# A Mamba scan layer and a Fourier layer on one core: the ends of the scan, and forward transforms by pairs of columns

## The chip, the cores and the metric

The kernel runs on one core of one Trainium2 chip. The metric is the device time of one execution in microseconds (us), as the median of several runs. A profile of one further execution gives the start and end of every instruction on the engines: PE (TensorE matmul; PEld is its weight load), DVE (VectorE), ACT (ScalarE), POOL (GpSimd) and SP (the queue that issues most DMAs).

## The reference

The input is x of shape 4 x 128 x 128 x 128 (image, channel, x, y), all float32. Layer 0 cuts each image into windows of 8 x 8 pixels, normalizes over channels, and runs a selective state-space scan over the 64 pixels of each window:

```python
t = x.reshape(B, C, nh, WS, nw, WS).transpose(0, 2, 4, 3, 5, 1).reshape(-1, L, C)
tn = (t - mu) * jax.lax.rsqrt(var + 1e-05) * ln_g + ln_b
xz = tn @ W_in + b_in
xi, z = (xz[..., :d_in], xz[..., d_in:])
xc = silu(sum((xp[:, k:k + L, :] * conv_w[:, k] for k in range(K))) + conv_b)
delta = jax.nn.softplus(dr @ dt_w + dt_b)
h = dA * h + (d_t * x_t)[:, :, None] * B_t[:, None, :]
y = jnp.einsum('nds,ns->nd', h, C_t)
```

Layer 1 normalizes again, takes a real two-dimensional Fourier transform, multiplies by conjugated filters, transforms back, mixes channels and ends in a small MLP:

```python
Xf = jnp.fft.rfft2(z, axes=(-2, -1))
Uf = Xf[:, :, None, :, :] * jnp.conj(Phi)[None, None]
U = jnp.fft.irfft2(Uf, s=(gx, gy), axes=(-2, -1))
S = jnp.einsum('bdlxy,lhd->bhxy', U, Theta)
```

## The kernel before

Four functions run one after another, joined by tensors in DRAM. All are scheduled by hand: each engine executes its instructions in the order in which the program text issues them, and the framework adds the waits that data and buffers need. DMAs are nearly all issued from SP's queue, which is in order too: a DMA that waits for its data or its buffer holds up all DMAs behind it.

**`mamba_layer` (from L34).** The 4 x 16 strips of 8 rows of pixels are called rows here, 64 in all. First come constants (L59 to L125): 17 loads over SP, the folding of the convolution into W_in (`W_conv`, L86 to L106) and of two projections into `W_dt` (L108 to L116), each through the only buffer of the PSUM tag `one`, and memsets of four `dA` tiles and `tn` on DVE. Then everything runs over slots `s` (L446): a row has U = 32 slots of the scan, one unit of 128 x 1024 elements in each, and its forward part starts LEAD = 30 slots ahead. The dictionaries `takes`, `makes` and `lates` say which helper runs in which slot. For the row that starts at `s`, these are the normalization of `xt` (`norm`, L293: matmul `ln_center`, ACT work `ln_scale`, matmul `ln_back`, ACT `f_affine`, for two halves in turn), convolutions and inputs (`f_conv`, `f_in`), Silu (`f_silu`, with a load of activation tables on either side), `f_dt`, `f_bc`, softplus (`f_soft`), the product `du`, and the stores of `delta` and `du` to DRAM, from which `fetch` loads replicated copies (`dr`, `ur`) for the scan. After the scan of a row come the gate, `b_out`, the store of `x1t`, a second normalization 89 slots after `s`, and the store of `z`.

PSUM has eight banks: three tiles of two banks under the tag `du` for the scan, one bank `y` for its sums, and the one bank `one`, through which every other matmul result passes.

For the first row nothing else runs while its forward part does; for the last row nothing else runs while its output and second normalization do.

**`spectra` (from L464).** For each of the four images: `along_x` (L493) multiplies, for each channel, a 128 x 128 plane `z` with the 128 columns of `fx` (cosines, then sines, of frequencies 0 to 64), four channels to a PSUM bank, and copies the bank into `a`, on ACT and DVE in turn. `z` arrives by tiles of 16 channels (512 KB) with three buffers, two loads ahead. Then `along_y` (L500) forms the spectrum column by column, three columns to a bank: column k needs the real part `a[:, m]` times one pair of blocks of `fy` and the imaginary part `a[:, WH + m]` times another, summed in PSUM, where m is k or 128 - k. Real and imaginary halves are then copied by ACT and DVE into `x`, 65 frequencies 512 bytes apart:

```python
nc.tensor.matmul(p2[:, o], a[:, m], fy[:, KY : 3 * KY], start=True, stop=single)
if not single:
    by = fy[:, : 2 * KY] if m == k else fy[:, 2 * KY :]
    nc.tensor.matmul(p2[:, o], a[:, WH + m], by, start=False, stop=True)
```

After each half of the 128 columns `x` (two buffers) is stored to `xf`, 4.26 MB (L527). The PSUM tags `p1` and `p2` have four banks each.

**`mix` (L530) and `images_and_mlp` (L616)** multiply by `phi` and `theta` and transform back. They read the constants `Phi_r`, `Phi_i` and `idft_x`, made in `layout` (L773) and `dft` (L745), in the order of the 128 columns.

Of the kernel before, what the change touches and what calls it, by code (L numbers as in the profile page):

```python
# [32 lines left out]

def mamba_layer(tc, d, x, x1, zb, deltas, dus):  # L34
# [18 lines left out]
    with ExitStack() as ctx:  # L53
# [4 lines left out]

        def load(name):  # L59
            t = cp.tile(list(d[name].shape), F32, tag=name, name=f"c_{name}")  # L60
            nc.sync.dma_start(t, d[name])
            return t
# [10 lines left out]
        names = "center rsel ssel ln_g ln_b W_in b_in conv_w conv_b W_bc dt_b A_log D W_out b_out gamma beta"  # L73
        c = {k: load(k) for k in names.split()}
        A = cp.tile([P, 32], F32, tag="A", name="A")
# [8 lines left out]
        fold = sb.tile([P, n], F32, tag="ab", name="fold")  # L84
        nc.sync.dma_start(fold[:, : 2 * P], d["W_in_t"])
        for ch in range(2):  # L86
            nc.vector.tensor_scalar(skip[:, ch], ident, c["D"][:, ch : ch + 1], None, ALU.mult)
            t = ps.tile([P, HB], F32, tag="one", name="p_fold")
            for k in range(K):
                diag = half(fold, 1)[:, k * P : (k + 1) * P]  # L90
                nc.vector.tensor_scalar(diag, ident, c["conv_w"][:, ch, k : k + 1], None, ALU.mult)
                w = fold[:, ch * P : (ch + 1) * P]
                nc.tensor.matmul(t[:, k * P : (k + 1) * P], w, diag, start=True, stop=True)
            nc.vector.tensor_copy(W_conv[:, ch].rearrange("p k m -> p (k m)"), t)

            b = c["b_in"][:, ch : ch + 1]
            sums = fold[:, 2 * P : 2 * P + K]
            nc.vector.tensor_copy(sums[:, :1], c["conv_w"][:, ch, :1])
            for k in range(1, K):
                nc.vector.tensor_tensor(sums[:, k : k + 1], sums[:, k - 1 : k], c["conv_w"][:, ch, k : k + 1], ALU.add)  # L100
            nc.vector.tensor_scalar(sums, sums, b, None, ALU.mult)
            for k in range(K - 1):
                nc.vector.tensor_scalar(
                    early[:, ch, :, k], sums[:, K - 2 - k : K - 1 - k].to_broadcast([P, WS]), -1.0, None, ALU.mult
                )
            nc.vector.tensor_tensor(b_conv[:, ch : ch + 1], sums[:, K - 1 :], c["conv_b"][:, ch : ch + 1], ALU.add)  # L106

        W_dt = cp.tile([P, 2, 2 * P], F32, tag="W_dt", name="W_dt")  # L108
        fold = sb.tile([P, n], F32, tag="ab", name="fold2")
        nc.sync.dma_start(fold[:DR, : 2 * P], d["W_xdt"])  # L110
        nc.sync.dma_start(fold[:DR, HB : HB + 2 * P], d["dt_w"])
        for ch in range(2):
            t = ps.tile([P, HB], F32, tag="one", name="p_fold")
            w = fold[:DR, ch * P : (ch + 1) * P]
            nc.tensor.matmul(t[:, : 2 * P], w, fold[:DR, HB : HB + 2 * P], start=True, stop=True)
            nc.vector.tensor_copy(W_dt[:, ch], t[:, : 2 * P])  # L116

        dAs = []
        for i in range(4):
            t = cp.tile([P, 2, WS, L], F32, tag=f"dA{i}", name="dA")  # L120
            nc.vector.memset(t, 0.0)
            dAs.append(t)

        tn = cp.tile([P, NW, K - 1 + L], F32, tag="tn", name="tn")
        nc.vector.memset(tn, 0.0)  # L125

        def one(name):
            return ps.tile([P, HB], F32, tag="one", name=name)

        rs = [SimpleNamespace(py={}, yz={}) for _ in rows_all]  # L130
# [14 lines left out]
        def ln_center(o, src, h):  # L145
            o.ln = one("ln_cen")
            for q in range(HB // P):
                at = h * HB + q * P
                tokens = getattr(o, src)[:, at : at + P]
                nc.tensor.matmul(o.ln[:, q * P : (q + 1) * P], tokens, c["center"], start=True, stop=True)  # L150

        def ln_scale(o):
            o.cs = sb.tile([P, HB], F32, tag="cs", name="cs", bufs=2)
            r = sb.tile([P, HB // P], F32, tag="ln_r", name="ln_r", bufs=2)
            blocks = [slice(q * P, (q + 1) * P) for q in range(HB // P)]
            for q, k in enumerate(blocks):
                nc.scalar.activation(o.cs[:, k], o.ln[:, k], AF.Square, accum_out=r[:, q : q + 1])

            nc.scalar.activation(r, r, AF.Ln, bias=eps, scale=1.0 / P)
            nc.scalar.activation(r, r, AF.Exp, scale=-0.5)  # L160
            for q, k in enumerate(blocks):
                nc.scalar.activation(o.cs[:, k], o.ln[:, k], AF.Copy, scale=r[:, q : q + 1])  # L162

        def ln_back(o):
            o.lb = one("ln_back")
            for q in range(HB // P):
                k = slice(q * P, (q + 1) * P)
                nc.tensor.matmul(o.lb[:, k], o.cs[:, k], ident, start=True, stop=True)  # L168


        def f_load(o, b, rows):
            o.xt = sb.tile([P, n], F32, tag="xt", name="xt", bufs=3)
            nc.sync.dma_start(o.xt, x[b, :, rows, :].rearrange("c i w -> c (i w)"))
# [119 lines left out]
        def norm(o, src, affine, at):  # L293
            for h in range(2):
                made(at + 2 * h, partial(ln_center, o, src, h), partial(ln_scale, o))
                made(at + 2 * h + 1, partial(ln_back, o), partial(affine, o, h))
# [3 lines left out]
        for r, (o, (b, rows)) in enumerate(zip(rs, rows_all)):  # L300
            s = U * r - LEAD
            for h in range(2):
                for k in range(2):
                    late(s + LEAD + 16 * h + 8 * k + 11, partial(b_gate, o, h, k))
                made(s + (61, 67)[h], partial(b_out, o, h), partial(b_out_bias, o, h))
            take(s + 72, partial(b_store, o, b, rows))
            norm(o, "x1t", b_affine, s + 89)
            take(s + 96, partial(b_store_z, o, b, rows))
        for r, (o, (b, rows)) in enumerate(zip(rs, rows_all)):
            s = U * r - LEAD  # L310
            take(s - 5, partial(f_load, o, b, rows))
            norm(o, "xt", f_affine, s - 1)
# [133 lines left out]
        for s in range(-LEAD - 5, U * R + 99 - LEAD):  # L446
            make, took = makes.get(s, ((), ()))
            go(takes.get(s, ()))
            fetch(s + 6)
            if s % 2:  # L450
                replicate(s + 1)
            else:
                total(s - 4)
            for q in range(2):
                decay(s + 2, q, True)
            for q in range(2):
                decay(s + 3, q, False)
            go(make)
            go(took)
            scan(s)  # L460
            go(lates.get(s, ()))


def spectra(tc, d, zb, xf):  # L464
# [10 lines left out]
    with ExitStack() as ctx:  # L475
# [3 lines left out]
        ps = ctx.enter_context(tc.tile_pool(name="f_ps", bufs=4, space=PSUM))  # L479
        fx = cp.tile([P, W], F32, tag="fx", name="fx")  # L480
        nc.sync.dma_start(fx, d["dft_x"])
        fy = cp.tile([P, 4 * KY], F32, tag="fy", name="fy")
# [4 lines left out]
        def load(b, i):  # L487
            b, i = b + i // P, i % P
            if b < B:
                loaded[b, i] = sb.tile([P, DG, W], F32, tag="z", name="z", bufs=3)  # L490
                nc.sync.dma_start(loaded[b, i], zb[b][i : i + DG].rearrange("c x y -> x c y"))

        def along_x(b, i, a):  # L493
            z = loaded[b, i - i % DG]
            p1 = ps.tile([P, CG, W], F32, tag="p1", name="p_fx")
# [3 lines left out]

        def along_y(a, x, cols):  # L500
            p2 = ps.tile([P, KG, 2 * KY], F32, tag="p2", name="p_fy")
            for o, k in zip(range(KG), cols):
                m = min(k, W - k)
                single = m % WH == 0
                nc.tensor.matmul(p2[:, o], a[:, m], fy[:, KY : 3 * KY], start=True, stop=single)
                if not single:
                    by = fy[:, : 2 * KY] if m == k else fy[:, 2 * KY :]
                    nc.tensor.matmul(p2[:, o], a[:, WH + m], by, start=False, stop=True)
            n, at = len(cols), cols[0] % WH
            for r in range(2):  # L510
                next(copies)(
                    x[:, :, r, at : at + n].rearrange("p y k -> p k y"), p2[:, :n, r * KY : (r + 1) * KY]
                )

        load(0, 0)
        load(0, DG)
        for b in range(B):
            a = sb.tile([P, W, P], F32, tag="a", name="a", bufs=1)
            for i in range(0, P, CG):
                if i % DG == 0:  # L520
                    load(b, i + 2 * DG)
                along_x(b, i, a)
            for q in range(2):
                x = sb.tile([P, KY, 2, WH], F32, tag="x", name="x")
                for k in range(q * WH, (q + 1) * WH, KG):
                    along_y(a, x, range(k, min(k + KG, (q + 1) * WH)))
                nc.sync.dma_start(xf[:, :, b, q].rearrange("y c r x -> c y r x"), x)  # L527
# [217 lines left out]
def dft():  # L745
# [7 lines left out]
        "dft_y": (h.imag, h.real, -h.imag, -h.real),  # L753
        "idft_x": (w.real, w.imag),
# [18 lines left out]
def layout(i):  # L773
# [17 lines left out]
    d["Phi_r"], d["Phi_i"] = (i[f"L1_conv_Phi_f_{k}"].transpose(1, 0, 2) for k in ("real", "imag"))  # L791
# [21 lines left out]
```

## Time and profile before

| what | us |
|---|---|
| median of three runs | 10317.22 (10314.53 to 10325.69) |
| the profiled execution | 10328.0 |
| its span, first to last instruction | 10326.2 |
| start of the first scan instruction | 107.06 |
| end of the last scan instruction | 7163.65 |
| issue of the last store of `z` | 7190.91 |
| issue of the last store of `xf` | 7602.14 |
| first matmul of the mix | 7628.4 |
| first matmul of the inverse transforms | 9529.0 |

So the scan layer takes some 7191 us, of which 107 before the first scan and 27 after the last, the forward transforms 411 to the issue of their last store, the mix some 1900 and the rest some 800. Over the whole span PE is busy for 9221.1 us (89%), DVE 8861.2 (86%), POOL 8141.9 (79%), ACT 6509.4 (63%). Such shares are averages over stages with different limits; a stage is read from its own stretch of the trace. In the groups of instructions that follow, a line holds the source line, the engine and operation, the tile written and the tiles read, the shape and count, then busy time in us and the mean of one in ns, and after it the idle time of that engine just before the group, with what ended it.

### The profile page before, as it was taken

The page shows a single profiled execution, that of the slowest core. Times are in us where ns is not written, and L with a number is a line of the kernel's source. Part 1 is how long each engine was busy: PE and PEld are TensorE (multiplying, and loading weights), DVE is VectorE, ACT ScalarE, POOL GpSimd, SP SyncE. Part 2 cuts the span into 40 slices and gives each one's busy share as a digit, 9 for nine tenths or more (in the row PEclk, how much of TensorE's full clock was granted, in tenths as well). Part 3 has the DMA queues.
Part 4 walks back from the last instruction along what each step waited for, and adds up shares of the span by engine and source line. Part 5 has one row for each costly group of instructions (what it writes and reads, how often), then busy time and mean ns, then how long its engine had stood idle before and what let it go on. Part 6 is the DMA issues. An engine that isn't in the chain of part 4 may idle for free.

```text
span 10326.2 us, 144410 instructions
## 1 busy us (share of the span) xinstructions
PE 9221.1 (89%) x48900; PEld 5007.4 (48%) x48900; DVE 8861.2 (86%) x7193; ACT 6509.4 (63%) x12439; POOL 8141.9 (79%) x4166
## 2 busy tenths in 40 slices
PE   6888888888888888888888888887889999998999
PEld 2333333333333333333333333333889999998766
DVE  5999999999999999999999999997359999998433
ACT  5777777777777776776776776775335555554433
POOL 5889999899899899899898899996039999996000
PEclk8999999999999999999999999997999999999999
DMA  4777777777777677677677777776531111112332
GB/s 141 222 219 220 220 221 219 217 222 219 217 225 221 212 232 218 212 230 219 211 227 220 210 227 220 214 226 183 154 103 38 38 38 38 38 38 62 138 127 94
DMA packets 1168115, 1794.11 MB, mean 174 GB/s; under 512 B 368640, under 2 KB 436496, under 8 KB 1166224
## 3 DMA queue, kind: packets, MB, share of 16 engines
q1 hardware_dynamic: 1167376, 1784.88, 57.1%
q8 instruction: 388, 6.36, 0.3%
q14 instruction: 351, 2.88, 0.1%
HBM read 1481.44 MB, written 303.04 MB: 173 GB/s over the span
## 4 chain that ended last, share of the span: by engine, by line
PE 65%; ACT 15%; DVE 8%; DMA 7%; issue 3%; SPq 1%; POOL 1%; DVEq 0%; ACTq 0%; POOLq 0%
PE p_v L564 18%; PE p_conv L202 6%; PE p_du L376 6%; DVE hs L410 5%; DMA dr<-delta 5%; PE p_dt L227 5%; PE p_bc L217 5%; PE p_y L428 5%; PE p_out L274 2%; DVE p_du L408 2%; ACT dA L391 2%; PE ln_cen L150 2%; ACT p_du L391 2%; PE p_h L686 2%; PE p_o L695 2%
## 5 line engine op out<-in xcount | busy, mean ns | idle before, releaser
L418 POOL TENSOR_TENSOR hs<-hs,bc 128x1024 f32<-128x1024 f32 x2048 | 4801.2, 2366 | 413.6 <-DVE hs L410 359.7
L410 DVE TENSOR_TENSOR_SCAN hs<-dA,p_du 128x1024 f32<-128x1024 f32 x1600 | 3659.0, 2287 | 208.6 <-DVE p_du L408 4.9
L581 POOL TENSOR_TENSOR acc<-acc,part 128x512 f32<-128x512 f32 x1408 | 1740.9, 1280 | 570.9 <-ACT part L579 565.9
L408 DVE TENSOR_TENSOR p_du<-p_du,bc 128x1024 f32<-128x1024 f32 x1600 | 1936.0, 1210 | 224.0 <-PE p_du L376 219.2
L391 ACT ACTIVATE dA<-dr,A 128x504 f32<-128x504 f32 x3200 | 2071.8, 704 | 32.9 <-DVE hs L410 23.3
L564 PE MATMUL p_v<-theta,xk 128*128 128x128 f32 x16640 | 1864.8, 275 | 31.5 <-DMA xk<-xf 27.0
L564 PEld LDWEIGHTS p_v<-theta,xk 128*128 128x128 f32 x16640 | 1861.9, 192 | 34.4 <-issue 27.2
L592 DVE SCALAR_TENSOR_TENSOR acc<-p_v,phi,acc 128x512 f32<-128x512 f32 x2622 | 1767.8, 743 | 105.4 <-PE p_v L564 80.9
L376 PE MATMUL p_du<-du,c_rsel 32*128 32x512 f32 x6400 | 1365.3, 678 | 369.9 <-DVE hs L410 369.9
L428 PE MATMUL p_y<-hs,c_ssel 128*32 128x512 f32 x8192 | 1223.7, 633 | 135.1 <-DVE yz L263 83.3
L579 ACT ACTIVATE part<-p_v,phi 128x512 f32<-128x512 f32 x1408 | 891.1, 686 | 578.7 <-PE p_v L564 572.0
L410 DVE TENSOR_TENSOR_SCAN hs<-p_du,ur 128x1024 f32<-128x1024 f32 x448 | 1019.0, 2275 | 87.1 <-ACT p_du L391 52.7
L356 POOL TENSOR_TENSOR ur<-ur,bc 128x1024 f32<-128x1024 f32 x448 | 1059.8, 2366 | 10.8 <-DMA ur<-du 10.8
L202 PE MATMUL p_conv<-tn,W_conv 128*128 128x512 f32 x2048 | 1010.8, 618 | 3.2 <-ACT xc L207 1.6
L376 PEld LDWEIGHTS p_du<-du,c_rsel 32*128 32x128 f32 x6400 | 370.7, 192 | 1081.0 <-issue 783.2
L227 PE MATMUL p_dt<-xc,W_dt 128*128 128x512 f32 x1024 | 620.3, 736 | 46.8 <-ACT dl L238 40.9
L391 ACT ACTIVATE p_du<-dr,A 128x504 f32<-128x504 f32 x896 | 613.8, 685 | 29.0
L428 PEld LDWEIGHTS p_y<-hs,c_ssel 128*32 128x32 f32 x8192 | 184.3, 111 | 890.3 <-issue 572.2
L207 ACT ACTIVATE xc<-p_conv,b_conv 128x512 f32<-128x512 f32 x256 | 176.2, 688 | 645.2 <-PE p_conv L202 645.2
L245 POOL TENSOR_TENSOR dl<-dl,ab 128x1024 f32<-128x1024 f32 x128 | 302.1, 2360 | 340.0 <-ACT ab L242 340.0
L202 PEld LDWEIGHTS p_conv<-tn,W_conv 128*128 128x128 f32 x2048 | 348.0, 190 | 457.5 <-issue 249.4
L168 PE MATMUL ln_back<-ident,cs 128*128 128x128 f32 x2048 | 339.5, 316 | 224.4 <-ACT cs L162 218.4
(99 smaller groups left out, 10104.8 us busy)
## 6 DMA issues: line engine op xcount, KB each, us to landing
dr<-delta SPq DMA_DIRECT2D x4096, 256.0 KB, 5.2
ur<-du SPq DMA_DIRECT2D x896, 256.0 KB, 6.4
delta<-dl SPq DMA_DIRECT2D x128, 512.0 KB, 2.9
du<-du SPq DMA_DIRECT2D x128, 512.0 KB, 5.2
xf<-x SPq DMA_DIRECT2D x8, 4160.0 KB, 16.4
xk<-xf SPq DMA_DIRECT2D x130, 256.0 KB, 3.7
sf<-acc SPq DMA_DIRECT2D x520, 64.0 KB, 1.7
s<-sf SPq DMA_DIRECT2D x8, 4160.0 KB, 12.6
```

Of the source, the lines that this page charges most:

```text
L202: nc.tensor.matmul(windows(o.pc), W_conv[:, ch, k], moved, start=(k == 0), stop=(k == K - 1))
L227: nc.tensor.matmul(o.pd, W_dt[:, k, ch * P : (ch + 1) * P], half(o.xc[:, k], h), start=(k == 0), stop=(k == 1))
L356: nc.gpsimd.tensor_tensor(fetched[s], fetched[s], both(o.bc[0], h), ALU.mult)
L376: nc.tensor.matmul(u.bank[:, j % 2], c["rsel"][p, u.i], half(u.o.du[p, u.ch], u.h), start=True, stop=True)
L391: nc.scalar.activation(u.dA[:, q, :, 1:], u.delta[:, q].rearrange("p (w t) -> p w t", t=L)[:, :, 1:], AF.Exp, scale=A[:, g : g + 1],)
L408: nc.vector.tensor_tensor(u.bu, u.bu, both(u.o.bc[0], u.h), ALU.mult)
L410: nc.vector.tensor_tensor_scan(u.hs.rearrange("p q t -> p (q t)"), u.dA.rearrange("p q w t -> p (q w t)"), u.bu.rearrange("p q t -> p (q t)"),
L418: nc.gpsimd.tensor_tensor(u.hs, u.hs, both(u.o.bc[1], u.h), ALU.mult)
L428: nc.tensor.matmul(o.py[h, ch][32 * j : 32 * j + 32], c["ssel"][:, u.i], units[s + j // 2].hs[:, j % 2], start=(u.i == 0), stop=False, ski ...
L564: nc.tensor.matmul(t[:, b], o.xk[:, b, r], theta[:, k], start=True, stop=True)
L581: nc.gpsimd.tensor_tensor(into, into, part, ALU.add)
L592: nc.vector.scalar_tensor_tensor(into, v, factor, into, ALU.mult, ALU.add)
```

## The change

Three things change.

*The start of the scan layer.* The activation table set that holds exp and ln is loaded as ACT's first instruction. The first row's tokens are loaded at the head of SP's queue; W_in_t, conv_w, b_in and conv_b are issued from ACT's queue; the other constants follow on SP in another order, with the two small matrices for `W_dt` (into a buffer of tag `z`) among them. The memsets of `dA` and `tn` go to POOL. The folds use the tag `du`. While no scan runs (`one.free`), `one()` hands out the first bank of a `du` tile, of which there are three. The first row's normalization centers both halves before either is turned back.

*The end of the scan layer.* The last row's second normalization goes to slots 68 to 71 after its `s`, both halves centered first, in place of 89 to 92, and its store of `z` to slot 72. `o.ln` and `o.cs` are kept by half. For all other rows the slots stay as they were.

*The forward transforms.* Columns m and 128 - m need the same products; one is the sum and the other the difference of the real part's and the imaginary part's. So for a pair each product is formed once, in two banks `pr` and `pi`; ACT copies `pi` and then `pr` to SBUF, DVE adds `pr` and the copy of `pi` into `x`, POOL subtracts the two copies into `x`. Columns 0 and 64 have one product and stand alone. The columns are stored in the order `COLS`, and `Phi_r`, `Phi_i` and `idft_x` are put in that order on the host. All PSUM tiles of the stage share one tag with eight banks; `z` has six buffers, with five loads ahead.

```diff
+COLS = np.arange(W // 2).reshape(2, 1, W // 4)
+COLS = np.concatenate((COLS, np.where(COLS > 0, W - COLS, W // 2)), 1).reshape(W)
...
+        nc.scalar.preload_act_table_set("natural_log_exp_and_others")
...
-            nc.sync.dma_start(t, d[name])
+            (nc.scalar if name in "conv_w b_in conv_b" else nc.sync).dma_start(t, d[name])
...
+        fold = sb.tile([P, n], F32, tag="ab", name="fold")
+        fold2 = sb.tile([P, n], F32, tag="z", name="fold2", bufs=2)
+        nc.scalar.dma_start(fold[:, : 2 * P], d["W_in_t"])
+        first = load_tokens(*rows_all[0])
+        names = "center ln_g ln_b conv_w b_in conv_b W_in D A_log dt_b W_bc rsel ssel W_out b_out gamma beta"
         c = {k: load(k) for k in names.split()}
+        nc.sync.dma_start(fold2[:DR, : 2 * P], d["W_xdt"])
+        nc.sync.dma_start(fold2[:DR, HB : HB + 2 * P], d["dt_w"])
...
-            t = ps.tile([P, HB], F32, tag="one", name="p_fold")
+            t = ps.tile([P, 2, HB], F32, tag="du", name="p_du", bufs=3)[:, 0]
...
-            nc.vector.memset(t, 0.0)
+            nc.gpsimd.memset(t, 0.0)
...
         def one(name):
+            if one.free:
+                return ps.tile([P, 2, HB], F32, tag="du", name="p_du", bufs=3)[:, 0]
             return ps.tile([P, HB], F32, tag="one", name=name)
...
-            norm(o, "x1t", b_affine, s + 89)
-            take(s + 96, partial(b_store_z, o, b, rows))
+            norm(o, "x1t", b_affine, *((s + k) for k in ((68, 69, 70, 71) if last else (89, 91, 90, 92))))
+            take(s + (72 if last else 96), partial(b_store_z, o, b, rows))
...
+            norm(o, "xt", f_affine, *((s + k) for k in ((-1, 0, 1, 2) if r == 0 else (-1, 1, 0, 2))))
...
         for s in range(-LEAD - 5, U * R + 99 - LEAD):
+            one.free = not -1 <= s < U * R
...
-        ps = ctx.enter_context(tc.tile_pool(name="f_ps", bufs=4, space=PSUM))
+        ps = ctx.enter_context(tc.tile_pool(name="f_ps", bufs=8, space=PSUM))
...
-                loaded[b, i] = sb.tile([P, DG, W], F32, tag="z", name="z", bufs=3)
+                loaded[b, i] = sb.tile([P, DG, W], F32, tag="z", name="z", bufs=6)
...
         def along_y(a, x, cols):
+            pr, pi = bank("p_fy_r"), bank("p_fy_i")
+            for o, m in enumerate(cols):
+                nc.tensor.matmul(pr[:, o], a[:, m], fy[:, KY:], start=True, stop=True)
+                nc.tensor.matmul(pi[:, o], a[:, WH + m], fy[:, : 2 * KY], start=True, stop=True)
...
+            def to(q):
+                at = q * (WH // 2) + cols[0] % (WH // 2)
+                return x[:, :, :, at : at + len(cols)].rearrange("p y r k -> p k r y")
...
+            imag = sb.tile([P, KG, 2 * KY], F32, tag="imag", name="imag", bufs=3)
+            real = sb.tile([P, KG, 2 * KY], F32, tag="real", name="real", bufs=3)
+            nc.scalar.copy(imag[:, : len(cols)], pi[:, : len(cols)])
+            nc.scalar.copy(real[:, : len(cols)], pr[:, : len(cols)])
+            nc.vector.tensor_tensor(to(0), parts(pr), parts(imag), ALU.add)
+            nc.gpsimd.tensor_tensor(to(1), parts(real), parts(imag), ALU.subtract)
...
+        for i in range(5):
+            load(0, i * DG)
...
-                    load(b, i + 2 * DG)
+                    load(b, i + 5 * DG)
                 along_x(b, i, a)
-            for q in range(2):
+            for h in range(2):
                 x = sb.tile([P, KY, 2, WH], F32, tag="x", name="x")
-                for k in range(q * WH, (q + 1) * WH, KG):
-                    along_y(a, x, range(k, min(k + KG, (q + 1) * WH)))
-                nc.sync.dma_start(xf[:, :, b, q].rearrange("y c r x -> c y r x"), x)
+                if h == 0:
+                    lone(a, x)
+                ms = range(max(1, h * (WH // 2)), (h + 1) * (WH // 2))
+                for k in range(0, len(ms), KG):
+                    along_y(a, x, ms[k : k + KG])
+                nc.sync.dma_start(xf[:, :, b, h].rearrange("y c r x -> c y r x"), x)
...
-        "idft_x": (w.real, w.imag),
+        "idft_x": (w.real[COLS], w.imag[COLS]),
```

The matmuls of columns 0 and 64, one each, with an ACT copy each, are in the new `lone(a, x)`.

## The prediction

> **What bounds the kernel now.** The forward transforms (`spectra`) carry most of the change, so the table of busy time by stretches was read there first (columns: stretch, length, then busy time and count of PE, PEld, DVE, ACT, POOL, granted PE clock, DMA share, GB/s):
>
> ```profile
> 7191.00:7233.00 42.00, 30.87 (x256) 30.39 (x256) 16.22 (x16) 16.66 (x16) 0.00 (x0) 0.85 0.91 263
> 7233.00:7291.00 58.00, 57.42 (x514) 57.45 (x515) 21.25 (x44) 21.32 (x44) 0.00 (x0) 1.00 0.28 78
> 7291.00:7336.00 45.00, 30.55 (x252) 30.20 (x251) 16.09 (x18) 16.66 (x16) 0.00 (x0) 0.85 0.96 271
> 7336.00:7394.00 58.00, 57.05 (x511) 57.08 (x512) 21.28 (x43) 21.12 (x44) 0.00 (x0) 1.00 0.29 83
> 7602.00:7628.00 26.00, 0.00 (x0) 0.00 (x0) 0.82 (x3) 0.00 (x0) 0.00 (x0) 0.59 0.96 272
> ```
>
> Each image has two parts: the transform along x (about 45 us, DMA full, PE two thirds busy) and along y (58 us, PE full, DMA idle, ACT and DVE a third busy, POOL without work). Second, the groups of instructions of that stage, shapes apart:
>
> ```profile
> L505 PE MATMUL p_fy<-fy,a 128*128 128x130 f32 x1024 | 197.0, 275 | 4.8 <-DVE a L498 4.8
> L508 PE MATMUL p_fy<-fy,a 128*128 128x130 f32 x1008 | 194.9, 275 | 0.0
> L511 ACT COPY x<-p_fy 128x195 f32<-128x195 f32 x168 | 83.5, 497 | 147.9 <-PE p_fy L508 147.9
> L511 ACT COPY x<-p_fy 128x65 f32<-128x65 f32 x8 | 2.2, 278 | 0.0
> L498 ACT COPY a<-p_fx 128x512 f32<-128x512 f32 x64 | 66.6, 1041 | 111.0 <-PE p_fx L497 111.0
> ```
>
> A matmul here is two passes (2032 for 1016 products), 0.1118 us apart (508 in 56.8 us). Third, its waits:
>
> ```profile
> DVE x L511 <- ACT x L511: 147.1, 168, 2.1
> PE p_fx L497 <- DMA z<-z: 53.8, 5, 14.3
> ```
>
> PE waits for the third `z` load of an image: 14.2 us before each of images 1 to 3, 10.5 before the first. Fourth, the chain that ended last, in order of time (start, us, what), at the start, at the end of the scan and into the transforms:
>
> ```profile
> 45.75 0.81 ACT tn L180
> ...
> 75.40 0.69 ACT zs L193
> ...
> 100.83 1.07 ACT ab L242
> 101.89 0.07 issue
> 101.96 2.35 POOL dl L245
> 104.33 0.34 SPq L254
> ...
> 7175.12 0.70 ACT x1t L280
> ...
> 7190.11 0.79 ACT z L288
> ...
> 7291.88 19.87 DMA z<-z
> ...
> 7602.14 16.10 DMA xf<-x
> ```
>
> Before the first scan (107.06) PE and ACT alternate through one PSUM bank. Last, two rows of the page price POOL:
>
> ```profile
> L418 POOL TENSOR_TENSOR hs<-hs,bc 128x1024 f32<-128x1024 f32 x2048 | 4801.2, 2366 | 413.6 <-DVE hs L410 359.7
> L581 POOL TENSOR_TENSOR acc<-acc,part 128x512 f32<-128x512 f32 x1408 | 1740.9, 1280 | 570.9 <-ACT part L579 565.9
> ```
>
> **What the Trainium skill says.** "GPSIMD Engine Reference", § 2.1, gives a two-input operation some 2.5 cycles per element, as both inputs share one read port; the rows above give (2366-1280)/512 = 2.12 ns per element and 0.195 us fixed, which agrees. Its § 1 has it contend with VectorE only where that is in a two-port mode or has two SBUF inputs; the new DVE add has one input in PSUM. "SBUF — State Buffer", under Door 1, has a penalty for each access that moves to another 16-byte line. The trace agrees: stores 512 bytes apart cost (497-278)/130 = 1.68 ns per element. "TensorE: Matmul & The Clock Gate", Part 1, has PE at half rate after an idle window; the trace agrees: eight passes of `ln_cen` take 2.08 us after idling and 1.16 when warm. "ScalarE: Activation LUTs", § Table sets, puts exp and ln into one named set; the trace shows a 1.28 us load ahead of each Ln and Exp of the first row, and none later, after that set's preload in `f_silu`.
>
> **The change part by part.**
>
> *Start.* The tokens go to the head of SP's queue; W_in_t, conv_w, b_in and conv_b move to ACT's queue, behind a 1.28 us table load and four issues of about 0.43 us there, ahead of A's Exp. Sixteen other loads follow the 512 KB of tokens on SP; A_log is issued near 3.5 instead of 5.91, and D likewise. So the first fold can start near 7.4 (before: 11.13, waiting for W_in_t, the 18th issue). From there to the end of the folds on DVE is 8.7 us as before; W_dt's two products no longer wait for loads that were issued only after the folds, and with three banks of the `du` ring PE runs through: last fold near 14.1, W_dt to 16.5, first `ln_cen` there or a little later (before 25.38). The five memsets leave DVE for POOL, which has nothing else until `dl`; a 128x128 memset there took 0.20 us, so five some 8 us at most, over before `tn` is first written near 25; they cost nothing unless they last past that.
> The two norm halves: cen 2.08, scale 2.96 twice on ACT (27.49 to 33.05 less two table loads of 1.28 and their gaps), the second cen and first back below them, back 2.08, affine 0.8: convolutions start near 27.5 instead of 46.61. Gain 19.
> Convolutions and inputs: before 29.5 us to 76.1, each 0.7 us of ACT between matmuls. With three banks PE alone counts: one cold convolution 7.1, three of 3.95, four inputs of 1.13, and a last copy: 24.1. Gain 5.4.
> After Silu (both table loads stay) p_dt and p_bc, 22.5 us from 79.36 to 101.9: PE 3.8 cold + 7 x 2.0, where `soft(1)` needs six of the eight, then ACT 1.3 + 2.1: 17.4. Gain 5.1. The store of the second delta, which holds SP's queue ahead of the fetches of `dr`, moves from 104.33 to about 75, and the scan with it: the fetches behind it keep their length. Sum 29, bounds 18 (if landing times or a cold PE take back a third) and 34.
>
> *Loop.* The slots of rows other than first and last come out the same; nothing is priced.
>
> *End.* x1t ends at 7175.82, the z store issues at 7190.91: 15.1 us, two halves in series. Now: cen 1.2, scale 2.95 twice, back 2.08, affine 0.8, gaps 0.1: 10.1. Gain 5. The z store moves up on SP to just behind the x1 store, of which it was always next; `fx`, `fy` and the first loads of `spectra` wait behind it as before.
>
> *Products along y.* Per image 63 pairs with two products each and two lone columns: 128 matmuls, 256 passes x 0.1118 = 28.6 us instead of 56.8. That holds only if evacuation is below 1.34 us per group of three pairs (12 passes):
> ACT, two contiguous copies of 390: "ScalarE: Activation LUTs", § What ACT_TABLE_LOAD costs, gives 186 + 0.833 x 390 = 511 ns, 93 overlapped; estimate 0.42 to 0.51 each, near the trace's 0.59 for 512. So 0.85 to 1.0.
> DVE, one add with scattered stores: 0.17 + 390 x 1.68 = 0.83. It waits for ACT's second copy too, since both read one bank, and behind it stand the next group's add and, at an image's end, copies of `a`; four groups fit into eight banks, so 2.3 us of latency holds nobody.
> POOL, one subtract: 0.195 + 390 x 2.12 = 1.02 if scattered stores cost it nothing. No POOL row of before stores scattered. From below: 1.02, as its reads are slower than the 1.68 ns of a scattered store on ACT and DVE. From above: both added, 390 x 3.8 + 0.2 = 1.68. I take 1.02; at 1.68 it adds 22 x 0.34 x 4 = 30 us.
>
> *Loads of z.* Six buffers and five loads ahead, so five of eight tiles are there when an image starts. The sixth is needed 5 x 3.58 = 17.9 us after (32 passes a tile). It stands on SP behind the x store of the second half, which waits for POOL's last subtract (about 2.3 after PE's end); a z load behind such a store took 19.87, so it lands at 22 to 24, later if the first half's store (16.4 us, issued 12.7 before) still drains. Stall 5, and up to 2.4 for a cold PE (192 passes took 23.9 instead of 21.5): 7.
> Period of an image: 28.6 + 7 + 1.4 (last copy of `a`) + 28.6 = 65.6 instead of 103.4: three times 37.8 = 113.5. First image: 9.4 to the first tile as before, 30.4 along x, 1.4, 28.6, 2.2 = 72 instead of 100.4: 28.4. End: last evacuation 1 us longer, and the first half's store may push the last by 1: -2. Sum 140. DMA needs 12.8 MB an image at 271 GB/s, 47 us: below 65.6.
>
> *The rest.* The order of columns changes only constants; the mix and the inverse keep their instructions.
>
> 29 + 5 + 140 = 174. The profiled execution took 10328.0 (span 10326.2, 1.8 around it), 11 us above the median of 10317.2; its stages stand in for the median's, so 10317.2 - 174 = **10143**.
>
> **Rivals.**
> *Evacuation takes PE's place.* For it: in the waits DVE's copies into `x` stood after ACT's 168 times; were DVE's add and POOL's subtract into one tile kept apart so, a group takes 0.83 + 1.02 + 0.1 = 1.95, 0.61 more: 54 us in all, 10197. Against: ACT's and DVE's interleaved stores into `a`, from different banks, overlap (ACT to 7206.11, DVE from 7205.96), so it was the shared bank.
> *The transfer stays late, or the scan's start is held by its own fetches.* The sixth tile stalls like the third before (16.6 instead of 7): 29 us, 10172. The lost start is as large. For it: DMA share 0.95 at 120 to 140. Against: the fetches only start after the delta store that moves.
> *Slower: scattered stores on POOL.* At `to(1)`, 8190 elements an image. It decides from 174/88 = 2 us more than 1.34 a group, 8 ns an element; at 10 ns a group takes 4.1 and the kernel 243 - 174 = 69 us longer, 10386. Against: ACT and DVE pay 1.68, both the same, as if SBUF set it.
> *Pairing does nothing*: would need PE not to bound 58 us at clock 1.00; hardly.
>
> **Numbers.** Forecast 0.62 (own range 10110 to 10168), evacuation 0.20, transfers or start 0.12, POOL slower 0.04, nothing 0.02. Range 10108 to 10205. 0.2% (21 us) is what can be told from no change: faster 0.94, same 0.02, slower 0.04.
>
> **What would show it.** Along y: near 29 us, PE full, POOL's subtract near 1.0 us and DVE's near 0.83; PE's wait for `z` three times about 5; first scan near 78; z store 10 us after x1t. Wrong: a POOL row above 1.35 us, POOL waiting for DVE on `x`, a later first scan, or a loop of other than 110 us a row.

## The result, and the profile after

| | median us (runs) | ratio to before, 95% interval |
|---|---|---|
| before | 10319.94 (4 runs, 10314.53 to 10325.69) | |
| changed | 10139.63 (4 runs, 10133.37 to 10142.77) | 0.9824 (0.9807 to 0.9841) |

The change saves 180 us. The forecast was 10143, with a range of 10108 to 10205.

Both profiled executions, cut at the same events (us):

| stage | before | after | gain | forecast |
|---|---|---|---|---|
| to the first scan | 107.1 | 71.8 | 35.3 | 29 |
| first to last scan start | 7054.3 | 7043.5 | 10.8 | 0 |
| last scan start to the load of `fx` | 30.0 | 23.6 | 6.4 | 5 |
| load of `fx` to the last `xf` store | 410.8 | 276.7 | 134.1 | 140 with the next |
| last `xf` store to the first `p_v` | 26.3 | 27.7 | -1.4 | |
| the rest | 2697.8 | 2695.6 | 2.2 | 0 |
| span | 10326.2 | 10138.9 | 187.3 | 174 |

The table by stretches over the first image and the second's transform along x (columns as in the prediction):

```profile
7138.00:7180.00 42.00, 30.90 (x256) 30.74 (x256) 16.50 (x16) 17.12 (x17) 0.00 (x0) 0.83 0.97 271
7180.00:7210.00 30.00, 29.23 (x259) 29.07 (x260) 16.65 (x22) 18.60 (x45) 19.95 (x20) 1.00 0.75 210
7210.00:7247.00 37.00, 30.89 (x255) 30.53 (x254) 17.39 (x18) 17.31 (x18) 1.73 (x2) 0.91 1.04 290
```

The part along y is 30 us instead of 58, with 256 passes in place of some 512, and PE is still full at clock 1.00: half of its work is gone and nothing took its place as the bound. DMA's share there rises from 0.28 to 0.75, since loads of `z` now run under it. The part along x is 37 us for the second image instead of 45.

The groups of the products along y and of their evacuation, shapes apart:

```profile
L527 PE MATMUL p_fy_r<-fy,a 128*128 128x130 f32 x504 | 98.5, 277 | 0.0
...
L543 POOL TENSOR_TENSOR x<-real,imag 128x390 f32<-128x390 f32 x80 | 82.2, 1028 | 208.8 <-ACT real L541 207.6 <-POOL x L543 1.2
...
L542 DVE TENSOR_TENSOR x<-p_fy_r,imag 128x390 f32<-128x390 f32 x80 | 68.1, 852 | 55.2 <-ACT real L541 52.9 <-POOL x L543 2.3
...
L541 ACT COPY real<-p_fy_r 128x390 f32<-128x390 f32 x80 | 39.3, 491 | 0.0
L540 ACT COPY imag<-p_fy_i 128x390 f32<-128x390 f32 x80 | 38.9, 486 | 41.5 <-issue 35.4 <-PE p_fy_i L528 6.2
```

All four durations stand where the prediction put them: POOL 1.03 us (1.02), DVE 0.85 (0.83), ACT 0.49 twice (0.42 to 0.51). Each engine's sum per group of three pairs is below PE's 1.34. DVE's idle time before the add was ended by ACT's second copy for 52.9 of its 55.2 us and by POOL for 2.3, so the two stores into one tile were hardly ever kept apart. The waits of the stage (total us, times, longest):

```profile
DVE x L542 <- ACT real L541: 52.9, 77, 5.3
...
PE p_fx L517 <- DMA z<-z: 26.9, 4, 10.6
```

PE's four waits for `z` sum to 26.9 us; the longest, 10.6, is the first image's. The other three take (26.9 - 10.6)/3 = 5.4 each, where 14.2 stood before. Last the chain in order of time (start, us, what):

```profile
70.45 0.34 SPq L269
...
7128.64 0.70 ACT x1t L295
...
7137.63 0.79 ACT z L303
...
7212.35 20.81 DMA z<-z
...
7233.30 13.17 PE p_fx L517 x96
...
7279.68 20.42 DMA z<-z
...
7348.92 20.74 DMA z<-z
...
7415.60 16.86 DMA xf<-x
```

The store of the second delta issues at 70.45 instead of 104.33. From the end of `x1t` (7129.34) to the `z` store (7138.43) there are 9.1 us instead of 15.1. The sixth `z` tile of the second image lands 20.81 us after its issue, and the 96 passes after that wait take 13.17 us instead of 96 x 0.1118 = 10.7: the first twenty or so come 0.213 us apart instead of 0.112. Such passes are called cold here.

### The profile page after: what moved, and what is told of

The parts are those of the page before. It is cut to its first block, busy times and chain, and to the rows that moved or that the text cites. A ratio compares the mean times of both kernels' runs of the same rounds, so it can differ in the third digit from the quotient of the medians.

```text
span 10138.9 us, 142594 instructions
## 1 busy us (share of the span) xinstructions
PE 9079.9 (90%) x47892; PEld 4881.8 (48%) x47892; DVE 8842.9 (87%) x7100; ACT 6494.8 (64%) x12443; POOL 8239.2 (81%) x4259
## 4 chain that ended last, share of the span: by engine, by line
PE 64%; ACT 15%; DVE 9%; DMA 6%; issue 3%; POOL 1%; SPq 1%; DVEq 0%; ACTq 0%; POOLq 0%
PE p_v L606 18%; PE p_conv L217 6%; PE p_du L395 6%; DVE hs L429 6%; DMA dr<-delta 5%; PE p_dt L242 5%; PE p_bc L232 5%; PE p_y L447 5%; DVE p_du L427 3%; PE p_out L289 2%; ACT dA L410 2%; PE ln_cen L166 2%; ACT cs L173 2%; ACT p_du L410 2%; PE p_h L728 2%
## 5 line engine op out<-in xcount | busy, mean ns | idle before, releaser
L606 PE MATMUL p_v<-theta,xk 128*128 128x128 f32 x16640 | 1863.5, 275 | 34.1 <-DMA xk<-xf 29.6
L375 POOL TENSOR_TENSOR ur<-ur,bc 128x1024 f32<-128x1024 f32 x448 | 1065.2, 2378 | 10.6 <-DMA ur<-du 10.6
L217 PE MATMUL p_conv<-tn,W_conv 128*128 128x512 f32 x2016 | 989.4, 615 | 0.0
L232 PE MATMUL p_bc<-xc,c_W_bc 128*128 128x512 f32 x1008 | 493.3, 612 | 36.0 <-ACT dl L253 36.0
```

Source lines behind the costliest of these rows:

```text
L217: nc.tensor.matmul(windows(o.pc), W_conv[:, ch, k], moved, start=(k == 0), stop=(k == K - 1))
L375: nc.gpsimd.tensor_tensor(fetched[s], fetched[s], both(o.bc[0], h), ALU.mult)
L606: nc.tensor.matmul(t[:, b], o.xk[:, b, r], theta[:, k], start=True, stop=True)
```

## The experiments

Stage times are from each run's profile, medians from repeated runs beside runs of before. All of a run's edits are against the changed kernel unless said otherwise. Seven early, one bank, no preload and both on POOL ran beside runs of before with a median of 10308.27 us; for the changed kernel and the others that median was 10319 to 10320.5. So medians of these two groups are compared here by what each saves against its own runs of before.

**Parts alone.** `e1_ends_only` has the new start and end of the scan layer with the old transforms; `e2_pairs_only` the old scan layer with the new transforms; `e4_before_again` is the kernel before, unchanged, profiled once more.

> Only the two ends of the scan layer changed; forward transforms as before. Theory (steps of the prediction, corrected by the trace of the changed kernel): first scan 35 us earlier, last z store 6 us sooner after the last scan, nothing else: 42 us less, 10278. First scan near 72 us, the stage of the transforms 411 us to its last store. Rival: the loop itself became faster through the change (11 us over 64 rows in the trace): 53 us less, 10267, with a loop some 7046 us long in this profile too.

> Scan layer as before, forward transforms by pairs. Theory: the gain of the transforms stands by itself: 277 us instead of 411 to the last store, 134 us less, 10186, and the loop as long as before within its own scatter. Rival: the transforms need the earlier end (tokens, buffers) for part of their gain: less than 120 us.

> The kernel before, unchanged, for a second profile. Theory: the scan loop (first to last scan, 7056.6 us in the first profile of before, 7045.8 in that of the changed kernel) scatters by about 10 us from execution to execution, so this one may lie anywhere from 7045 to 7065. Rival: the loop is fixed by the program, so it is 7056.6 within 2 us.

| run | first scan | loop | to `fx` | transforms | median us | ratio (95%) |
|---|---|---|---|---|---|---|
| ends only | 73.4 | 7038.3 | 23.2 | 410.8 | 10270.85 | 0.9957 (0.9941 to 0.9974) |
| pairs only | 105.7 | 7036.4 | 30.0 | 276.6 | 10187.92 | 0.9868 (0.9854 to 0.9883) |
| before again | 107.0 | 7044.3 | 31.1 | 410.0 | 10318.01 (one run) | |

The ends give 48 us and the pairs 131, together 179: the two parts add up to the whole. The 48 lie between the theory's 42 and the rival's 53. In the profile of the ends alone the two stages at the ends are 33.6 and 6.8 us shorter than before, 40.4 in all; the other 8 us are in neither. The loop took 7036.4 with the old scan layer and the new transforms, 7044.3 and 7054.3 in two profiles of one and the same program, and 7034.2 to 7048.5 in the eleven profiles with the new scan layer. So the loop's 10.8 us in the first table is no more than one program scatters by; a difference of a few us in the loop is not excluded.

**Buffers of `z`.** `e3_z_three`:

```diff
-loaded[b, i] = sb.tile([P, DG, W], F32, tag="z", name="z", bufs=6)
+loaded[b, i] = sb.tile([P, DG, W], F32, tag="z", name="z", bufs=3)
-for i in range(5):
+for i in range(2):
-load(b, i + 5 * DG)
+load(b, i + 2 * DG)
```

> Changed kernel, but z with three buffers and two loads ahead as before. Theory: the third tile of images 1 to 3 is again needed 7.2 us after the start and lands 21 to 24 after it, so PE waits 14 to 17 us instead of 5.4: 27 to 35 us more, 10167 to 10175. Rival: the wait is set by the volume of the stores and not by the order of issue, so that more buffers did nothing: 10140.

The wait of its stage (total us, times, longest):

```profile
PE p_fx L517 <- DMA z<-z: 60.6, 7, 16.3
```

The stage takes 310.9 us instead of 276.7 and the median is 10175.47 (0.9860, 0.9845 to 0.9875). The waits for `z` rise by 60.6 - 26.9 = 33.7, which is the whole difference of 34.2: the deeper ring is worth as much as the waits it removes.

**One more tile before the store.** `e8_sixth_early` and `e12_seven_early` move the late load to the other side of the `xf` stores on SP's queue. The first keeps six buffers, issues six first loads and puts an image's last load ahead of its products along y; the second does the same with seven buffers:

```diff
 e8_sixth_early
-for i in range(5):
+for i in range(6):
-    if i % DG == 0:
+    if i and i % DG == 0:
         load(b, i + 5 * DG)
     along_x(b, i, a)
+load(b, P + 5 * DG)
 e12_seven_early
-tag="z", name="z", bufs=6)
+tag="z", name="z", bufs=7)
-for i in range(5):
+for i in range(7):
-    if i % DG == 0:
-        load(b, i + 5 * DG)
+    if i and i % DG == 0:
+        load(b, i + 6 * DG)
     along_x(b, i, a)
+load(b, P + 6 * DG)
```

> Changed kernel, with the sixth z load of the next image issued right after the transform along x, ahead of both stores on SP's queue, same six buffers. Theory: the stall of 5.4 us and the cold passes behind it (2.5 us) go at images 1 to 3, but the seventh tile, needed 21.5 us after the start, lands at 22 to 24 behind the store: 1 to 2 us of stall remain, 15 to 20 us less, 10120 to 10125. Rival: the loads only push the stores back and PE waits as long for the seventh tile: 10140.

> Changed kernel with seven z buffers and seven of eight loads issued ahead of the stores. Theory: the eighth tile is needed 25 us after an image's start and lands at 22 to 24, so the stall goes at images 1 to 3: another 8 to 12 us off the stage against six loads (261.9 us to its last store there), 250 to 254, the whole near 10115 to 10123. Rival: the stage is held by the volume of its transfers and stays at 262.

| run | transforms | waits for `z` in all | median us | ratio (95%) |
|---|---|---|---|---|
| changed | 276.7 | 26.9 | 10139.63 | 0.9824 (0.9807 to 0.9841) |
| six early | 261.9 | 18.0 | 10133.27 | 0.9817 (0.9802 to 0.9831) |
| seven early | 255.3 | 10.5 | 10111.34 | 0.9808 (0.9793 to 0.9823) |

The waits of the version with seven buffers:

```profile
PE p_fx L517 <- DMA z<-z: 10.5, 1, 10.5
```

Only the first image's wait is left. The stage falls by 21.4 us. Along x the three later images gain 24.2: 16.2 of waits and 8.0 of the cold passes that followed each wait. The stretch with the second image's first products has clock 1.00 where the changed kernel had 0.91, and the stretch after it, which is its part along y, has 0.94:

```profile
7200.00:7230.00 30.00, 28.34 (x253) 27.98 (x251) 17.36 (x18) 17.08 (x18) 1.15 (x2) 1.00 1.03 291
7230.00:7260.00 30.00, 30.00 (x254) 30.00 (x255) 16.43 (x20) 17.84 (x43) 19.84 (x20) 0.94 0.95 266
```

So cold passes are not all gone. In images 2 to 4 of this run the part along y begins with some and takes 31.2 us instead of 29.6; the changed kernel has this in its third image alone. It takes back 3.3 us, and no run shows why it comes.

All four runs (10109.09 to 10113.58) lie below every run of both kernels, but the runs of before beside them were lower too. Seven early saves 197 us and the changed kernel 180, and the intervals of the two ratios overlap. Its profile also has the lowest loop time of all runs (7034.2), so of its gain only the stage's 21.4 us is put down to the edit. With six early the stage gives 14.8 us, just short of the 15 to 20 expected, and the median only 6; the loop's scatter is large enough to hide the difference.

**One pool of eight banks.** `e5_banks_apart` gives `p_fx` four banks of its own and the pairs four:

```diff
-ps = ctx.enter_context(tc.tile_pool(name="f_ps", bufs=8, space=PSUM))
+ps = ctx.enter_context(tc.tile_pool(name="f_ps", bufs=4, space=PSUM))
-p1 = ps.tile([P, HB], F32, tag="p", name="p_fx")
+p1 = ps.tile([P, HB], F32, tag="p1", name="p_fx")
```

> Changed kernel with four PSUM banks for the transforms along x and four for the pairs, instead of one pool of eight. Theory: two groups of pairs in flight; a bank is read to its end 1.95 us after PE's last pass into it, against 1.34 us of PE work in the other group, so two groups take 3.29 us instead of 2.68: 0.3 a group, 88 groups, 27 us more, 10167. Rival: two groups suffice, as before the change with four banks: 10140.

Of PE's timeline along y (start, us, line, tile, passes, and in brackets the idle time before and its releaser), two of the waits:

```profile
7199.11 0.49 PE L528 MATMUL p_fy_i<-fy,a 128*128 128x130 f32 x2 [0.32 <-DVE x L542]
...
7202.36 0.49 PE L528 MATMUL p_fy_i<-fy,a 128*128 128x130 f32 x2 [0.31 <-DVE x L542]
```

Two groups come every 3.25 us (7199.11 to 7202.36), where PE alone needs 2.68: with two groups in flight PE waits for DVE's add, the last reader of `pr`. Of the 88 groups 80 have three pairs, so that is 40 x 0.57 = 23 us; 1.1 us of it per later image comes back at `z` (23.6 of waits instead of 26.9). The stage takes 296.1, 19.4 more, and the median is 10164.28 (0.9851, 0.9834 to 0.9867). Two groups in flight are too few and the four that eight banks hold are enough, as the prediction reckoned; three were not tried.

**Order and engine of the evacuation.** `e6_real_first` swaps ACT's two copies. `e7_both_on_dve` takes POOL's work away and lets DVE add and subtract, with only the imaginary products copied; `e11_both_on_pool` gives POOL both:

```diff
 e6_real_first
-nc.scalar.copy(imag[:, : len(cols)], pi[:, : len(cols)])
 nc.scalar.copy(real[:, : len(cols)], pr[:, : len(cols)])
+nc.scalar.copy(imag[:, : len(cols)], pi[:, : len(cols)])
 e7_both_on_dve
-nc.gpsimd.tensor_tensor(to(1), parts(real), parts(imag), ALU.subtract)
+nc.vector.tensor_tensor(to(1), parts(pr), parts(imag), ALU.subtract)
 e11_both_on_pool
-nc.vector.tensor_tensor(to(0), parts(pr), parts(imag), ALU.add)
+nc.gpsimd.tensor_tensor(to(0), parts(real), parts(imag), ALU.add)
```

> Changed kernel with the copies of ACT the other way round, real products first. Theory: four groups are in flight, so 0.5 us more or less of waiting in a group reaches nobody: within 3 us of the changed kernel, 10140. Rival: the order lets DVE and POOL start sooner and so carries part of the gain: 10 us more or above.

> Changed kernel with the subtraction on DVE, from PSUM, and without ACT's copy of the real products. Theory: evacuation takes PE's place: DVE needs 2 x 0.85 us and a gap, 1.75 a group instead of PE's 1.34, 0.41 x 88 = 36 us more, 10176, with PE waiting for DVE along y. Rival: PE still bounds the stage: 10140.

> Changed kernel with the addition on POOL as well, from the two copies in SBUF. Theory (the prediction's rival of evacuation taking PE's place, with a price known now): two operations of 1.03 us, of which a few hundredths overlap, are 2.0 a group against PE's 1.34: 0.66 x 88 = 58 us more, 10198, ACT and PE waiting for POOL along y. Rival: PE still bounds the stage: 10140.

| run | transforms | median us | ratio (95%) |
|---|---|---|---|
| real first | 275.4 | 10139.91 | 0.9824 (0.9810 to 0.9839) |
| both on DVE | 276.0 | 10142.40 | 0.9827 (0.9812 to 0.9841) |
| both on POOL | 327.6 | 10183.77 | 0.9879 (0.9862 to 0.9895) |

The order of the copies is worth nothing (the stage differs by 1.3 us). With both on DVE my theory failed. Two operations of 0.85 us seemed to make 1.7 per group, above PE's 1.34; nothing was lost. The timeline of DVE shows why (start, duration):

```profile
7195.61 0.86 DVE L541 TENSOR_TENSOR x<-p_fy_r,imag 128x390 f32<-128x390 f32 x1
7196.30 0.86 DVE L540 TENSOR_TENSOR x<-p_fy_r,imag 128x390 f32<-128x390 f32 x1
```

They start 0.69 apart: each lasts 0.86, and its last 0.17 lies under the next. Two make 1.38, about PE's pace. So POOL's subtraction and ACT's second copy, with which the change begins to use a fourth engine, are not needed for its gain. The same view of the run with both on POOL:

```profile
7194.23 1.06 POOL L542 TENSOR_TENSOR x<-real,imag 128x390 f32<-128x390 f32 x1
7195.20 1.07 POOL L543 TENSOR_TENSOR x<-real,imag 128x390 f32<-128x390 f32 x1
```

Here the starts lie 0.97 apart, 1.94 a group: above 1.34 by 0.60, and 80 groups x 0.60 = 48 us without the eight shorter ones, against 50.9 measured in the stage. Less than half of it shows along y, where PE takes 33.8 to 35.3 us an image instead of 29.6, since the banks let it run ahead of POOL. POOL ends 11 us after PE, the store of `x` waits for POOL and the next load of `z` waits behind the store, so PE's waits for `z` are 48.7 us instead of 26.9. In these runs the largest of the engines' sums per group decides: 1.94 costs about what it exceeds PE's 1.34 by, and 1.38 costs nothing that shows.

**The start.** `e9_one_bank` leaves `one()` a single bank outside the loop too; `e10_no_preload` drops the load of the table set at the head of ACT:

```diff
 e9_one_bank
-one.free = not -1 <= s < U * R
+one.free = False
 e10_no_preload
-nc.scalar.preload_act_table_set("natural_log_exp_and_others")
```

> Changed kernel, with every matmul result outside the scan through one PSUM bank again (the folds keep theirs). Theory: the three banks carry most of the earlier start: convolutions and inputs take 29.5 us again instead of 21.3, p_dt to the last softplus 22.5 instead of 15.7, the two norm halves some 3 more; first scan 15 to 18 us later, at 87 to 90, and the end 1 to 3 us longer: 10156 to 10160. Rival: earlier loads and the table set carry it, and the first scan moves by less than 8 us.

> Changed kernel without the table set's load at the start. Theory: four table loads of 1.28 us come back into the first row's norm, one after another on ACT, 5.1 us, and nothing hides them: first scan near 77, 10145, which the median can hardly tell. Rival: they run while ACT waits for PE or a load: first scan within 2 us of 71.8.

With one bank the first scan starts at 93.9 instead of 71.8, and from the last scan to `fx` 30.0 us pass, as in the kernel before (30.0): without the three banks 22.1 of the start's 35.3 us are lost, more than the 15 to 18 I had reckoned, and all of the end's gain. The last row's earlier slots and the order of its halves are as in the changed kernel here, so they bring nothing by themselves; the banks without them were not tried. The median is 10162.79 (0.9856, 0.9842 to 0.9871), 146 us saved instead of 180. Its chain shows PE and ACT alternating again (start, us, what):

```profile
80.00 2.00 PE p_dt L242 x4
...
82.77 0.59 ACT dl L253
...
83.40 2.00 PE p_dt L242 x4
```

Without the preload the table loads between Ln and Exp return, four of them; in ACT's timeline (start, duration) the first and the last:

```profile
20.98 1.28 ACT L173 ACT_TABLE_LOAD   x1
...
27.92 1.28 ACT L174 ACT_TABLE_LOAD   x1
```

The first scan is 5.4 us later (77.2), about 4 x 1.28 = 5.1. The median, 10141.14 (0.9836, 0.9821 to 0.9851), saves 167 us instead of 180, and the intervals of the two ratios overlap: so small a part can be read in its own stage only.

## Why the prediction was right

*Products along y.* The step was right in mechanism and size: 128 matmuls an image, PE full, every evacuation sum below 1.34 us. The one cost that before did not show, POOL's scattered store, came at its lower bound. The slower rival needed 3.3 us a group; POOL took 1.03.

*Transforms as a whole.* The term was 140 and measured 134.1 - 1.4 = 132.7. The period of an image was put at 65.6 us. From one late `z` load to the next in the chain it is 67.3 (7212.35 to 7279.68) and 69.2 (7279.68 to 7348.92), and 67.3 for the last image, from `xf` store to `xf` store. That is 7 us in sum. The stall itself was right (5 forecast, 5.4 measured). The cold passes behind it were taken from the old stage as up to 2.4 and cost 2.4 (13.17 - 10.7) to 3.1 (13.80 - 10.7). Of the rest, some 1 us an image is the part along y, which takes 29.6 and not 28.6 even at full clock; half of that is PE's wait for the first ACT copy of a lone column (1.9 us in four images). Another 1.7 is the third image's part along y, 31.2 us at clock 0.95.

*The start.* Forecast 29, measured 35.3, from the profile. The main mechanism is the one named, PE and ACT in turn through one bank. Mis-sized was the step "With three banks PE alone counts": its 24.1 us for convolutions and inputs measured 21.3 (27.74 to 49.06), and its 17.4 for `p_dt` and `p_bc` 15.7. I had added durations from a stretch where each step waited for the one before. Such a duration holds latency that work standing in line pays only once: a convolution that stood alone took 3.95 us and one in line 3.65, a `p_dt` 2.0 and 1.80. That the latency is the cause is argued from these pairs of numbers; no run isolates it.

One step of the start is wrong in mechanism: that the store of the second delta holds up the first scan. The first scan waits for ACT's `dA`, and that for a fetch of `dr`:

```profile
70.19 1.51 ACT L410 ACTIVATE dA<-dr,A 128x504 f32<-128x504 f32 x2 [1.23 <-DMA dr<-delta]
71.79 2.29 DVE L429 TENSOR_TENSOR_SCAN hs<-dA,p_du 128x1024 f32<-128x1024 f32 x1 [1.36 <-ACT dA L410]
```

The fetch was issued at 66.39, behind the first delta, and `dA` starts at 70.19, before the second delta's store at 70.45. Store and scan both moved by some 34 to 35 us, so the wrong step did little harm to the number. From the end of softplus to the first scan 3.8 us pass instead of 5.2. That gain of 1.4 was not in the forecast.

*Loads at the start.* The folds were to begin near 7.4 and began at 9.38. The loads that precede them on SP are not free: its queue stood for 2.5 us until the tokens had landed.

In the waits, by total us, times and longest:

```profile
SPq L67 <- DMA xt<-in_x_dram: 2.5, 1, 2.5
```

The gains elsewhere in the start were larger than this loss.

*End.* 5 forecast, 6.4 measured, and all of it is lost in the run with one bank.

*Loop.* Priced at nothing, and the runs show nothing beyond scatter: two profiles of the kernel before differ by nearly as much (10.0 us) as the profiles of before and after do (10.8), and the kernel with the old scan layer and the new transforms has 7036.4. So the profiled span's 187.3 us is some 10 too large as a measure of the change; the medians' 180 is nearer, and is what 174 stands against.

*The sum.* The three terms came to 35.3 + 6.4 + 132.7 = 174.4, where 174 was forecast. That it fits so closely is luck: the start gave 6.3 more and the end 1.4 more than forecast, the transforms 7.3 less.

*Rivals.* Evacuation as the bound did not occur, but the run with both on POOL shows that it is real, at 1.94 us a group. The late transfer is half true: 5.4 us of wait and some 2.7 of cold PE remain for three images, and a seventh buffer with the earlier load removes them from the part along x. The scan's start is held by its own fetch, as the rival said, but for 1.23 us and not for 29.

## What to carry over

When several engines evacuate what one produces, sum each engine's start-to-start distance per group and compare it with the producer's time: what stayed below it here was free, another order of the copies brought nothing, and the banks had only to cover the latency. Before adding buffers, look at which transfers stand ahead of a late load on its queue: here one load moved ahead of two stores took 14.8 us off a stage of 277 without another buffer. Read a gain of a few microseconds in its own stage, since a long loop elsewhere can scatter by ten.

## What the runs showed of the hardware

- With work in line an engine starts an operation before the record of the one before it ends: DVE's add of 390 elements lasts 0.86 us and starts every 0.69; POOL's lasts 1.07 and starts every 0.97.
- POOL's two-input operation of 390 elements takes 1.028 us with stores 512 bytes apart, where contiguous ones of 512 took 1.280 before: both lie within 1% of 0.195 us + 2.12 ns per element. Stores 512 bytes apart, at which copies by ACT and DVE took 1.68 and 1.79 ns per element (195 against 65 elements in the kernel before), cost POOL nothing that shows.
- DVE and POOL wrote interleaved elements of one tile at once, and neither slowed the other: DVE's add took 0.852 us beside POOL and 0.847 without it, POOL's operation 1.028 beside DVE and 1.036 without it. "GPSIMD Engine Reference" of the Trainium skill, § 1, has them contend only where VectorE is in a two-port mode or has two SBUF inputs; here it has one, and the trace agrees.
